# The sampling of the last five tiles: sums of weighted windows as matrix products with the identity, and another order of the last slots

## The chip, the cores and the metric

The kernel runs on one core of one Trainium2 chip, as a single launch. Its time is device microseconds (us), the median of three runs: 3848.34 us (3845.51 to 3851.66). The engines of the core that matter here are TensorE (PE in the profile, with its weight loads as PEld), VectorE (DVE), ScalarE (ACT), GpSimd (POOL) and SyncE (SP, which issues most of the DMAs). Each engine works through its own queue in order.

## The reference

The input is an image batch x of 4 x 64 x 64 pixels with 256 channels, in float32. Layer 0 is self-attention over the 4096 pixels of each image. Layer 1 is a block with deformable 3x3 sampling and an MLP:

```python
# layer 0
attention = softmax(q @ k.T);  x = gamma * (attention @ v) + x
# layer 1
h  = ln(x);  x_proj = h @ inproj_w + inproj_b
x1 = gelu(ln(depthwise3x3(h)))
offset, mask = x1 @ off_w + off_b, softmax(x1 @ mask_w + mask_b)   # per pixel: 16 groups, 9 points
val = bilinear samples of x_proj at (pixel + point + offset)
x = x + (sum over points of val * mask) @ outproj_w + outproj_b
x = x + gelu(ln(x) @ fc1_w + fc1_b) @ fc2_w + fc2_b
```

## The kernel before

A tile is 128 pixels (two image rows) with all 256 channels; there are 128 tiles. Attention works in 64 units of two tiles (b, u; UN = 64). The rest of layer 1 works in 65 pieces v = 0 to 64 (PN = 65): pieces 0 and 64 have one tile, all others two, so the last three pieces, 62, 63 and 64, have five tiles together.

The bilinear samples are not gathered one by one. As long as offsets stay within one pixel, each pixel's samples lie in a 5 x 5 window of x_proj. `plan` computes, for each pixel, window position and group, the weight `wn`. `sample` (line 1034) then computes, for each of a tile's five window rows r:

- `rows` (1039): SP loads the window row from DRAM, 128 pixels x 5 columns x 256 channels, unless an earlier tile loaded it; six such buffers exist;
- `times` (1042, product at 1047): DVE multiplies the window row by its weights, 128 x 1280 elements. Row 0 goes into a buffer with the tag "acc" (one of them), rows 1 to 4 into buffers with the tag "add" (two of them);
- `plus` (1054): DVE adds row r's product to row 0's, 128 x 1280 elements, four times a tile;
- `across` (1057): three DVE adds of 512, 256 and 256 elements per partition fold the five columns into `sp`, 128 x 256. At the end of a piece SP stores `sp` to `spd`.

`back` is the end of layer 1, in `finish` (line 1080): `turn` transposes `sp` on TensorE, `copy` (ACT), `project_out` (TensorE), `added` (DVE), `stats`, `shift`, `norm`, `turn2`, `scale`, then `hidden0` to `hidden7` (four matrix products each) with a `gelu` each on ACT, `narrowed0` and `narrowed1` (16 matrix products each, line 1141), and `end` (DVE, 1147), which also starts the store of the output. One more such round, `far` (1203), handles single points with large offsets, and `checks` tests whether a second pass is needed.

The order of the work is written out by hand. Slots are numbered; `WHEN` (324) gives each step a number within its slot, `LATE` (390) overrides it for the last slots (59 to 66), and `whole` (1326) sorts all steps by 60 x slot + number and emits them in this order. Each of TensorE, DVE, ACT and POOL then executes its instructions in exactly this order; SP's order is not fixed in this way. The numbers only set an order, they are not times. Piece v has its sampling and its back in slot v + 2, so pieces 62 to 64 belong to slots 64 to 66.

All results of TensorE that go through the PSUM tag "m" (transposes, products of `finish`, `plan` and `front`) share two buffers. Attention's scores use four PSUM buffers of their own, "e0" to "e3" (`e_tile`, 670), which are last used by the last attention unit.

Of the kernel before, what the change touches and what calls it, by code (L numbers as in the profile page):

```python
# [16 lines left out]
def tile_attention_dcnv3_block(  # L17
# [293 lines left out]
    def transposed(src, name, n=2, pool=None, tag="m"):  # L311

        pt = (pool or ps).tile([P, C // P, 256], F32, tag=tag, name=f"pt_{name}")
        for k in range(C // P):
            for i in range(n):
# [69 lines left out]
            "range": 12.0, "left": 12.1, "largest": 12.2,  # L385
# [6 lines left out]
            60: {"e2": 41.49, "w7": 44.5, "x2": 48.96, "w6": 49.61, "e3": 59.92, "w10": 62.77, "w4": 73.03,  # L392
                "x3": 83.29, "w11": 85.02, "w8": 89.86, "w12": 91.45, "w14": 94.26, "w13": 95.34,
                "w9": 113.4, "w15": 117.14},
            61: {"load": -3.2, "e0": 45.5, "x0": 51.27, "e1": 59.9, "x1": 71.66, "w0": 73.04, "w1": 76.59,
                "e2": 80.2, "w4": 82.06, "w3": 82.78, "x2": 83.76, "w10": 83.88, "w2": 86.39, "w7": 92.1,
                "w6": 100.44, "e3": 102.52, "w9": 103.15, "x3": 103.68, "w5": 104.24, "w12": 110.82,
                "w11": 114.27, "w14": 115.93, "w13": 116.02, "w8": 117.01, "w15": 117.71},
            62: {"load": 53.63, "e0": 66.06, "x0": 73.02, "e1": 78.84, "w0": 88.05, "w3": 100.69,
                "w2": 103.2, "x1": 106.97, "w5": 108.02, "w6": 113.39, "e2": 116.3, "w4": 117.55,  # L400
                "x2": 119.12, "w9": 122.0, "w1": 124.07, "e3": 124.61, "w10": 125.61, "w11": 131.23,
                "x3": 131.69, "w8": 135.71, "w13": 135.92, "w14": 137.46, "w12": 137.48, "w7": 138.87,
                "w15": 142.25},
            63: {"load": 45.22, "e0": 89.67, "x0": 91.49, "e1": 92.19, "w0": 98.07, "x1": 98.39, "w7": 99.54,
                "w1": 104.93, "e2": 104.94, "w3": 106.18, "w4": 108.57, "w2": 110.23, "x2": 111.63,
                "w9": 113.71, "e3": 117.35, "w11": 117.47, "x3": 117.74, "w12": 120.69, "w8": 121.81,
                "w13": 124.71, "w14": 130.05, "w5": 130.64, "w6": 131.24, "w10": 133.48, "w15": 135.85},
        },
        "sample": {
            60: {"rows14": 42.14, "rows13": 59.29, "across00": 61.86, "across01": 62.94, "across02": 65.9,  # L410
                "rows11": 71.88, "times11": 71.89, "rows10": 72.53, "times10": 72.54, "plus11": 73.67,
                "rows12": 73.82, "times12": 73.83, "times14": 79.95, "plus12": 81.1, "times13": 87.36,
                "plus13": 87.92, "plus14": 88.59, "across10": 90.04, "across11": 91.66, "across12": 96.83},
            61: {"rows04": -3.66, "rows03": 24.5, "rows14": 41.53, "rows00": 70.98, "times00": 70.99,
                "rows01": 71.16, "times01": 71.17, "rows02": 73.82, "times02": 73.83, "plus01": 79.14,
                "plus02": 80.53, "times03": 85.26, "times04": 85.98, "plus03": 86.15, "rows12": 91.45,
                "times12": 91.46, "plus04": 93.4, "across00": 99.51, "rows13": 100.36, "across01": 102.53,
                "across02": 108.03, "rows11": 112.36, "times11": 112.37, "rows10": 113.32, "times10": 113.33,
                "plus11": 114.34, "plus12": 118.64, "times13": 122.27, "times14": 123.0, "plus13": 126.65,
                "plus14": 129.62, "across10": 134.07, "across11": 141.77, "across12": 144.34},  # L420
            62: {"rows14": 72.21, "rows00": 117.68, "times00": 117.69, "rows03": 117.71, "rows01": 119.28,
                "times01": 119.29, "plus01": 121.78, "rows02": 124.59, "times02": 124.6, "rows04": 126.03,
                "plus02": 126.5, "times03": 126.6, "times04": 128.12, "plus03": 128.47, "plus04": 130.31,
                "rows11": 130.32, "times11": 130.33, "across00": 132.44, "across01": 135.0,
                "across02": 137.38, "rows10": 140.82, "times10": 140.83, "rows12": 141.57, "times12": 141.58,
                "plus11": 142.3, "times14": 145.21, "plus12": 150.77, "rows13": 152.98, "times13": 157.69,
                "plus13": 159.16, "plus14": 161.51, "across10": 165.15, "across11": 167.74,
                "across12": 169.62},
            63: {"rows13": 102.75, "rows04": 104.25, "rows00": 110.64, "times00": 110.65, "rows03": 112.68,
                "rows01": 114.51, "times01": 114.52, "rows02": 114.67, "times02": 114.68, "plus01": 115.3,  # L430
                "plus02": 119.19, "times03": 119.59, "times04": 121.51, "plus03": 121.85, "rows14": 125.54,
                "plus04": 128.4, "across00": 130.89, "rows12": 132.38, "across01": 132.39, "times12": 132.4,
                "rows11": 132.41, "times11": 132.42, "across02": 134.36, "rows10": 135.11, "times10": 135.12,
                "plus11": 137.85, "plus12": 145.42, "times13": 145.49, "times14": 146.33, "plus13": 149.57,
                "plus14": 150.93, "across10": 160.15, "across11": 162.44, "across12": 174.56},
            64: {"rows04": 62.71, "rows03": 94.46, "rows13": 135.97, "rows01": 136.98, "times01": 136.99,
                "rows00": 139.55, "times00": 139.56, "plus01": 142.22, "times03": 142.61, "rows02": 144.59,
                "times02": 144.6, "plus02": 145.58, "plus03": 151.96, "times04": 152.08, "rows11": 154.09,
                "times11": 154.1, "plus04": 154.11, "across00": 155.61, "rows12": 159.49, "times12": 159.5,
                "across01": 161.77, "across02": 171.41, "rows14": 175.68, "rows10": 177.57,  # L440
                "times10": 177.58, "plus11": 178.21, "times14": 179.49, "plus12": 179.56, "times13": 185.46,
                "plus13": 190.08, "plus14": 212.44, "across10": 220.75, "across11": 222.25,
                "across12": 230.44},
            65: {"rows14": 94.03, "rows03": 116.37, "rows04": 151.89, "rows00": 177.78, "times00": 177.79,
                "rows01": 179.39, "times01": 179.4, "plus01": 187.51, "rows02": 189.46, "times02": 189.47,
                "times03": 191.56, "plus02": 195.53, "plus03": 203.22, "times04": 205.67, "rows12": 213.72,
                "times12": 213.73, "plus04": 222.18, "across00": 222.92, "across01": 225.43, "rows13": 226.4,
                "across02": 230.02, "rows11": 231.43, "times11": 231.44, "rows10": 234.3, "times10": 234.31,
                "plus11": 236.93, "plus12": 241.12, "times13": 242.24, "times14": 247.32, "plus13": 248.9,
                "plus14": 251.64, "across10": 260.73, "across11": 267.14, "across12": 281.03},  # L450
            66: {"rows03": 182.99, "rows04": 183.57, "rows01": 292.3, "times01": 292.31, "rows00": 299.77,
                "times00": 299.78, "rows02": 302.28, "times02": 302.29, "plus01": 318.35, "plus02": 332.49,
                "times03": 351.38, "times04": 358.89, "plus03": 363.72, "plus04": 364.57, "across00": 372.87,
                "across01": 376.88, "across02": 380.09},
        },
        "plan": {
            60: {"tap3": 42.84, "tap4": 46.73, "tap5": 51.03, "tap6": 51.93, "tap7": 59.16, "tap8": 60.74,
                "turn": 60.98, "stats": 61.98, "shift": 66.63, "norm": 67.13, "turn2": 68.17, "gelu": 69.98,
                "heads0": 78.28, "bias0": 78.87, "heads1": 85.48, "bias1": 85.66, "hat0": 86.22,
                "hat2": 86.52, "mask_exp": 87.01, "hat1": 87.37, "sums": 88.24, "invert": 88.67,  # L460
                "nearer": 89.94, "weigh": 91.59, "near": 96.38, "carry": 96.51, "mask0": 97.55,
                "product0": 105.33, "y_copies0": 107.13, "mask1": 109.87, "y0": 114.77, "product1": 114.97,
                "y1": 120.64, "y_copies1": 123.19, "x_copies": 123.89, "x": 125.57, "count": 150.62,
                "bounds": 186.94},
# [569 lines left out]
    def sample(v, wns, sps):  # L1034
# [7 lines left out]
        def times(i, r):  # L1042
            if i == 0 and r == 0:
                sps[v] = p1.tile([P, 2, C], F32, tag="sp", name=f"sp_{n}")[:, :nt]
# [405 lines left out]
```

## Time and profile before

| | before |
|---|---|
| median of three runs | 3848.34 us |
| the profiled execution, its own time | 3846.97 us |
| its span in the trace | 3845.0 us |
| PE busy, instructions | 3770.7 us (98%), 20316 |
| DVE busy, instructions | 3421.7 us (89%), 6224 |
| ACT busy, instructions | 2201.8 us (57%), 4258 |
| L1047, products of `times` | 640 of 1485 ns |
| L1055, adds of `plus` | 512 of 1485 ns |

The span runs from the first to the last instruction of the profiled execution; its own time is 1.97 us longer. "Busy" is the time in which an engine has an instruction in it. Matrix products overlap in TensorE's pipeline, so their mean duration is longer than the distance from one to the next; where a product's price is wanted, it is read from the starts of a row of them.

### The profile page before, as it was taken

How to read it: one execution, taken by the hardware profiler on the slowest of the kernel's cores; microseconds unless marked ns; L12 is line 12 of the kernel's file. 1: busy time of each engine (PE TensorE's matmuls, PEld its weight loads, DVE VectorE, ACT ScalarE, POOL GpSimd, SP SyncE). 2: the span in 40 equal slices, each digit the busy share in tenths (PEclk: the TensorE clock that was granted, in tenths of full speed). 3: DMA queues.
4: the chain of work that ended last, by engine and by line, in shares of the span. 5: the costliest groups of instructions: out<-in, count | busy, mean ns of one | idle time of the engine just before them, and what ended most of it. 6: DMA issues, size and time to landing. Idle time of an engine off the chain costs nothing. (4 is left out here: it accounts for less than half of the span.)

```text
span 3845.0 us, 55916 instructions
## 1 busy us (share of the span) xinstructions
PE 3770.7 (98%) x20316; PEld 3117.3 (81%) x20316; DVE 3421.7 (89%) x6224; ACT 2201.8 (57%) x4258; POOL 317.6 (8%) x444
## 2 busy tenths in 40 slices
PE   8999999999999999999999999999999999999977
PEld 7788888888888888888888888888888888888755
DVE  2599899999999998998998998998999999999997
ACT  4556556556555565565565565565565566565533
POOL 1000000000000000000000000000000000000020
PEclk9999999999999999999999999999999999999979
DMA  5333333334343333333543333333343333332321
GB/s 150 91 104 89 94 101 90 96 94 137 99 110 95 97 91 94 100 94 88 150 111 91 106 91 91 104 89 95 106 123 102 95 87 92 87 94 75 99 79 51
DMA packets 231788, 378.01 MB, mean 98 GB/s; under 512 B 32880, under 2 KB 181936, under 8 KB 231504
## 3 DMA queue, kind: packets, MB, share of 16 engines
q1 hardware_dynamic: 221408, 367.46, 34.2%
q10 hardware_dynamic: 8512, 3.43, 0.4%
q8 instruction: 162, 2.65, 0.3%
q0 software_dynamic: 1584, 3.47, 0.3%
q14 instruction: 122, 1.00, 0.1%
HBM read 251.69 MB, written 122.56 MB: 97 GB/s over the span
## 5 line engine op out<-in xcount | busy, mean ns | idle before, releaser
L727 PE MATMUL acc<-V,ex 128*128 128x257 f32 x8192 | 1901.1, 382 | 1.6 <-ACT ex L715 1.5
L727 PEld LDWEIGHTS acc<-V,ex 128*128 128x128 f32 x8192 | 1532.1, 190 | 266.6 <-issue 65.5
L1047 DVE TENSOR_TENSOR pw<-win,wn 128x1280 f32<-128x1280 f32 x640 | 933.4, 1485 | 7.2 <-ACT wn L991 1.1
L1055 DVE TENSOR_TENSOR pw<-pw,pw 128x1280 f32<-128x1280 f32 x512 | 760.5, 1485 | 0.1
L715 ACT ACTIVATE ex<-e 128x512 f32<-128x512 f32 x1024 | 529.2, 602 | 65.3 <-PE e L702 60.7
L1124 PE MATMUL ph<-hT_b,f1w 128*128 128x256 f32 (+1 forms) x2080 | 498.8, 383 | 11.3 <-ACT gT L1132 7.5
L1141 PE MATMUL pmlp<-f2w,gT 128*128 128x256 f32 x2048 | 463.0, 379 | 0.3 <-DVE om L877 0.3
L1124 PEld LDWEIGHTS ph<-hT_b,f1w 128*128 128x128 f32 x2080 | 384.5, 191 | 91.2 <-issue 15.5
L831 DVE SCALAR_TENSOR_TENSOR cv<-hs,dw,cv 128x256 f32<-128x256 f32 (+1 forms) x1076 | 429.2, 466 | 7.9 <-ACT cv L827 1.3
L1141 PEld LDWEIGHTS pmlp<-f2w,gT 128*128 128x128 f32 x2048 | 384.1, 190 | 51.2 <-DVE om L877 0.8
L1132 ACT ACTIVATE gT<-ph,f1b 128x256 f32<-128x256 f32 (+1 forms) x520 | 236.9, 468 | 263.0 <-PE ph L1124 260.3
L288 ACT ACTIVATE xn_p<-pc,nm_p,rstd_p 128x256 f32<-128x256 f32 x128 | 65.5, 561 | 539.0 <-DVE nm_p L280 539.0
L702 PE MATMUL e<-qs,kT 32*128 32x256 f32 x4096 | 297.1, 401 | 0.7 <-ACT ex L715 0.7
L702 PEld LDWEIGHTS e<-qs,kT 32*128 32x128 f32 x4096 | 187.1, 184 | 72.7 <-issue 63.3
L715 ACT ACT_TABLE_LOAD x185 | 237.4, 1283 | 3.1
L274 POOL TENSOR_SCALAR rstd_p<-mv_p 128x2 f32<-128x2 f32 (+1 forms) x65 | 76.2, 1173 | 1700.4 <-DVE mv_p L272 1665.4
L868 PE MATMUL po<-om_w,ge 128*128 128x432 f32 x512 | 197.6, 528 | 0.7 <-ACT ge L861 0.7
L957 DVE TENSOR_TENSOR pr<-hat 128x1296 f32<-128x1296 f32 x128 | 192.7, 1506 | 0.7 <-DVE nm_b L280 0.5
L1132 ACT ACT_TABLE_LOAD x124 | 159.1, 1283 | 6.4 <-PE ph L1124 4.2
L861 ACT ACTIVATE ge<-pt_p,bd,gd 128x256 f32<-128x256 f32 (+1 forms) x130 | 66.0, 559 | 157.8 <-PE pt_p L316 157.8
L877 DVE TENSOR_TENSOR om<-po,om_b 128x432 f32<-128x432 f32 x128 | 77.3, 605 | 87.9 <-PE po L868 87.9
L868 PEld LDWEIGHTS po<-om_w,ge 128*128 128x128 f32 x512 | 97.7, 191 | 70.9 <-issue 64.0
(215 smaller groups left out, 3823.6 us busy)
## 6 DMA issues: line engine op xcount, KB each, us to landing
win<-xp SPq DMA_DIRECT2D x536, 320.0 KB, 4.1
omd<-om SPq DMA_DIRECT2D x63, 432.0 KB, 2.5
xs<-in_x_dram SPq DMA_DIRECT2D x64, 256.0 KB, 5.4
x<-in_x_dram SPq DMA_DIRECT2D x64, 256.0 KB, 2.7
x1d<-x SPq DMA_DIRECT2D x64, 256.0 KB, 3.2
xp<-xq SPq DMA_DIRECT2D x128, 128.0 KB, 2.4
x1b<-x1d SPq DMA_DIRECT2D x63, 256.0 KB, 2.8
spd<-sp SPq DMA_DIRECT2D x63, 256.0 KB, 2.1
```

The source lines that it names most:

```text
L702: nc.tensor.matmul(es[r][:, jj, :], lhsT=self.kT[2 * g + jj][rows4(r), :], rhs=self.qs[rows4(r), :], start=True, stop=not self.general,)
L715: nc.scalar.activation(ex, self.es[r], AF.Exp)
L727: nc.tensor.matmul(self.acc[i], lhsT=ex[:, jj, i * P : (i + 1) * P], rhs=V[t // 2][:, t % 2, :], start=(g == 0 and r == 0 and jj == 0), st ...
L831: nc.vector.scalar_tensor_tensor(dst, src, dw[:, k, j : j + 1], dst, ALU.mult, ALU.add)
L868: nc.tensor.matmul(st["po", i], lhsT=st["ge"][:, k, i * P : (i + 1) * P], rhs=om_w[:, k, :], start=(k == 0), stop=(k == 1),)
L877: nc.vector.tensor_add(st["om"][:, i, :], st["po", i], om_b)
L957: nc.vector.tensor_mul(pr.rearrange("p a b c d g -> p a b (c d g)"), hat[:, :, i, 1, :].unsqueeze(1).to_broadcast([P, 3, 3, S]), hat[:, :, ...
L1047: nc.vector.tensor_mul(st[r].rearrange("p d (g c) -> p (d g) c", c=GC), src.rearrange("p d (g c) -> p (d g) c", c=GC), wns[v][:, i, r] .re ...
L1055: nc.vector.tensor_add(st[0], st[0], st[r])
L1124: nc.tensor.matmul(ph[:, :m], lhsT=f1w[:, k, c * P : (c + 1) * P], rhs=st["hT"][:, k, :m], start=(k == 0), stop=(k == 1),)
L1132: nc.scalar.activation(st["gT"][:, c, :m], st["ph", c][:, :m], AF.Gelu, bias=f1b[:, c : c + 1])
L1141: nc.tensor.matmul(po, lhsT=st["gT"][:, c, i * P : (i + 1) * P], rhs=f2w[:, c, :], start=(c == 0), stop=(c == NH - 1),)
```

## The change

For pieces 62, 63 and 64 (`v >= UN - 2`), the sums over the window are made in another way. Of the five products of a tile, rows 1 and 2 are added on DVE in place (`pair`, j = 1), and so are rows 3 and 4 (`pair`, j = 3). The three row buffers that are left (1, 0 and 3), each of five columns, are added by TensorE: `sum_up` multiplies each column by the identity and accumulates all 15 products in one PSUM tile, which uses one of attention's score buffers. ACT copies the result to `sp` (`summed`). `plus` and `across` are not called for these pieces. Their steps have a stage of their own, "summing". In `times`, `sp` is now allocated at the first call for a piece, whichever row that is.

```diff
         def times(i, r):
-            if i == 0 and r == 0:
+            if v not in sps:
                 sps[v] = p1.tile([P, 2, C], F32, tag="sp", name=f"sp_{n}")[:, :nt]
...
+        def pair(j):
+            nc.vector.tensor_add(st[j], st[j], st[j + 1])
+
+        def sum_up(i, j):
+            if j == 1:
+                st["sum", i] = ps_e.tile([P, 2, C], F32, tag=f"e{2 * (v % 2) + i}", name=f"sum_{n}_{i}")[:, 0, :]
+            for d in range(WIN):
+                nc.tensor.matmul(
+                    st["sum", i], lhsT=ident, rhs=st[j][:, d, :],
+                    start=(j == 1 and d == 0), stop=(j == 3 and d == WIN - 1),
+                )
+
+        def summed(i):
+            nc.scalar.copy(sps[v][:, i, :], st["sum", i])
+            if i == nt - 1:
+                nc.sync.dma_start(spt_[:, g0 : g0 + nt], sps[v])
+
         d = {}
+        if v >= UN - 2:
+            for i in range(nt):
+                for r in range(WIN):
+                    d[f"rows{i}{r}"] = lambda i=i, r=r: rows(i, r)
+                    d[f"times{i}{r}"] = lambda i=i, r=r: times(i, r)
+                for j in (1, 3):
+                    d[f"pair{i}{j}"] = lambda j=j: pair(j)
+                for j in (1, 0, 3):
+                    d[f"sum{i}{j}"] = lambda i=i, j=j: sum_up(i, j)
+                d[f"summed{i}"] = lambda i=i: summed(i)
+            return d
...
-            put(v + 2, "sample", sample(v, wns, sps))
+            put(v + 2, "sample" if v < UN - 2 else "summing", sample(v, wns, sps))
```

The second part replaces nearly the whole of `LATE`: every stage of slots 59 to 66 gets new numbers, so the order of all steps in the last slots changes, attention's included. As an example, here are the numbers of piece 63's sampling (slot 65) and of the checks:

```diff
-            65: {"rows14": 94.03, "rows03": 116.37, "rows04": 151.89, "rows00": 177.78, "times00": 177.79,
-                "rows01": 179.39, "times01": 179.4, "plus01": 187.51, "rows02": 189.46, "times02": 189.47,
...
+            65: {"rows04": 101.89, "rows03": 178.02, "rows13": 232.6, "rows02": 250.39, "times02": 250.4,
+                "rows01": 254.69, "times01": 254.7, "pair01": 261.82, "rows14": 262.32, "rows00": 267.01,
+                "times00": 267.02, "times03": 267.13, "sum01": 267.42, "times04": 270.89, "sum00": 283.46,
+                "pair03": 287.04, "rows11": 288.53, "times11": 288.54, "sum03": 294.71, "rows12": 320.51,
+                "times12": 320.52, "pair11": 346.58, "sum11": 348.47, "rows10": 353.1, "times10": 353.11,
+                "times14": 354.54, "sum10": 357.52, "times13": 357.91, "pair13": 358.79, "summed0": 364.31,
+                "sum13": 364.33, "summed1": 367.57},
...
-            66: {"range": 395.84, "left": 485.76, "largest": 510.45},
+            66: {"range": 530.02, "left": 563.34, "largest": 1080.93},
```

Sorted, the new order of TensorE from piece 63's last sum to the end is: the sum; `turn` of far and of 63; `project_out` of far and of 63; `narrowed0` and `narrowed1` of 62; `turn2`, eight `hidden`, `narrowed0` and `narrowed1` of 63; `turn2` of far; the first sum of the last tile; two `hidden` of far; the second sum; two `hidden` of far; the third sum; one `hidden` of far; `turn` of 64; one `hidden` of far; `project_out` of 64; two `hidden`, then `narrowed0` of far; `turn2`, eight `hidden` and `narrowed0` of 64; `largest` of the checks. Before, `largest` (two small products) stood between `turn2` and the first `hidden` of 64.

## The prediction

> **What bounds the kernel now.** I read the page first (PE 98% busy, DVE 89%), then the busy time by stretches, cut where the work changes: the last attention product ends at 3668.1 us, the last sum of the last tile's sampling at 3815.5.
>
> ```profile
> core 0: us, PE busy (x) PEld busy (x) DVE busy (x) ACT busy (x) POOL busy (x), PEclk, DMA share, GB/s
> 3500.00:3600.00 100.00, 100.00 (x550) 82.47 (x552) 94.50 (x175) 51.27 (x103) 10.81 (x12) 1.00 0.31 84
> 3600.00:3668.10 68.10, 65.61 (x345) 52.29 (x337) 66.59 (x114) 39.38 (x69) 6.47 (x7) 1.00 0.32 86
> 3668.10:3815.50 147.40, 105.24 (x420) 79.58 (x419) 140.67 (x288) 54.93 (x121) 24.21 (x26) 0.84 0.27 77
> 3815.50:3845.00 29.50, 18.89 (x96) 14.71 (x94) 5.79 (x24) 9.89 (x24) 1.89 (x3) 0.84 0.06 19
> ```
>
> While attention runs, PE is full. In the third stretch, where all five changed tiles are sampled, DVE is idle for only 6.7 us of 147.4, PE for 42.2, at a mean clock of 0.84. In the last stretch PE leads again. So DVE time taken out of the third stretch is worth its full length, as long as PE keeps up there.
>
> **What goes from DVE.** The timeline of DVE shows start, duration and line; the price of an instruction is the distance to the next start.
>
> ```profile
> 3787.19 0.69 DVE L1060 TENSOR_TENSOR pw<-pw 128x512 f32<-128x512 f32 x1
> 3787.79 0.60 DVE L949 TENSOR_TENSOR hat<-hat,mk 128x432 f32<-128x432 f32 x1
> 3788.31 0.42 DVE L1062 TENSOR_TENSOR pw<-pw 128x256 f32<-128x256 f32 x1
> 3788.64 0.69 DVE L1113 TENSOR_TENSOR x1b<-x1b,f2b 128x512 f32<-128x512 f32 x1
> 3789.24 0.42 DVE L1064 TENSOR_TENSOR sp<-pw 128x256 f32<-128x256 f32 x1
> 3789.58 1.51 DVE L957 TENSOR_TENSOR pr<-hat 128x1296 f32<-128x1296 f32 x1
> ...
> 3804.54 1.49 DVE L1055 TENSOR_TENSOR pw<-pw,pw 128x1280 f32<-128x1280 f32 x1
> 3805.94 0.19 DVE L932 TENSOR_TENSOR least<-least,ms 128x32 f32<-128x32 f32 x1
> ```
>
> The `across` adds cost 0.60 + 0.33 + 0.34 = 1.27 us a tile, one `plus` 1.40. A tile has five products before and after; four `plus` and three `across` become two `pair` of the same size as `plus`. Saved: 2 x 1.40 + 1.27 = 4.07 us a tile, 20.4 us for five.
>
> **What comes to PE.** Fifteen products a tile, 75 in all, 128x256 in float32, the form of L1141 and L1099. Timeline of PE, with the idle time before a row in brackets:
>
> ```profile
> 3687.89 3.78 PE L1099 MATMUL pout<-ow,sT 128*128 128x256 f32 x8
> ...
> 3776.39 5.45 PE L1124 MATMUL ph<-hT_b,f1w 128*128 128x256 f32 x24 [1.85 <-ACT gT L1132]
> 3781.68 7.07 PE L1141 MATMUL pmlp<-f2w,gT 128*128 128x256 f32 x32
> 3788.59 0.27 PE L316 MATMUL pt_s<-ident,sp 128*128 128x128 f32 x1
> ```
>
> Thirty-two products from 3781.68 to 3788.59 are 0.216 us each, so five columns cost 1.08 us and all 75 cost 16.2. But the eight at 3687.89, which start 1.6 us after an idle time of 6.3 us (DVE's sum was late), take until 3691.47, 0.447 each. [...] I take 0.216 for the sums after the fourth gap below and count one half-rate period after each gap of 4 us or more.
>
> Does it fit? In the third stretch PE's products at 0.216 (and in proportion to their columns) come to about 86 us; the other 19 of the 105 busy are low clock. With the 16.2, and with `narrowed` steps that the new order sorts ahead of the last sum, PE has about 104 to 108 us of work up to that sum, and DVE 140.7 - 20.4 = 120.3. PE is slack on average, not everywhere.
>
> **The walk through the new order.** I sorted the steps and added the prices above on both engines.
>
> - Up to the end of attention both orders hold nearly the same: 168.9 us of PE steps against 170.9 from the same start. Worth up to 2 us, counted as 0, because DVE, which is 98% busy from 3600 on, decides what follows.
> - From 3668 to piece 63's last sum DVE leads. Between the same point of piece 61's sampling (done at 3668.5) and piece 63's last `pair`, DVE has 101 us of work; with 2 us of idle time that `pair` ends at 3771. On the way PE has waits of about 5 us (for the last attention tile's norm), 4 us (for 63's taps) and 4 us (for 64's norm). The half clock after the first two costs PE's slack alone. After the third, about 3748, it would push on DVE.
> - From 3772 PE leads. Its queue from there to the end, from the rows: turns and projections 3.3, two `narrowed` 6.9, turn 0.4, eight `hidden` 7.2, two `narrowed` 6.9, turn 0.2, three sums 3.2, far's `hidden` 4.6, turn and projection 1.1, far's `narrowed` 3.5, turn 0.2, `hidden` 4.7, `narrowed` 3.7: 46 us. DVE, with some 27 us of work up to the last tile's `pair`, must wait in between: its `end` of 63 stands ahead of the last `times`, and 63's `narrowed` isn't done before 3797.
>
> The last rows of the chain of waits (start, length) give the prices of that tail:
>
> ```profile
> 3798.71 7.20 PE ph L1124 x32
> ...
> 3821.60 5.42 PE pmlp_f L1141 x16
> ...
> 3832.84 3.69 PE pmlp L1141 x16
> ```
>
> PE's small waits after 3797 sum to 3.4 us before (for ACT copies, norms, gelu tables); I keep 3.4. So PE ends at 3772 + 46 + 3.4 = 3821.4, against 3836.5: **15.1 us earlier**. What follows it (0.4 us `end`, the store, about 8 us to the end of the span) stays.
>
> **Edits with a small price.** (1) ACT gets five copies of 128x256; the row of the same form (L1093) has 0.37 us, 1.9 in all. ACT is 37% busy there; only the last one is on the path, but three `across` (1.27) leave it, so copy plus last five products (1.08 + 0.37) is about even. (2) Waits added on DVE: "add" has two buffers; after each `pair` the second next product needs the buffer that the `sum` still reads, nine times in all; the single "acc" buffer likewise waits for the middle sum. Behind the waiting product stand all of DVE's taps, norms and `end`s. The new order leaves 1.7 us (63's row 2, second tile) to several us between `pair` and that product, against 1.08 for the sum: from 0 to 9 x 1 us; I take 1, as most have 3 us. (3) PSUM: the sums use attention's score buffers, free by then; nothing. (4) `largest` moves from ahead of the last eight `hidden` to the end: 0.6 us leave the path (inside the 15.1), and its answer comes some 1.5 us after the last `end`, beside the output's store, which takes 3.0 us to land: nothing; 1 us if that cover is gone. (5) Loads of windows: every new one is requested before or as soon as one of six buffers is read out, on SP, which has 4.3 us median to landing; 62's row 4 is the tightest: its buffer comes free with row 1's product, some 9 us of DVE work ahead of its use. Cost 0 to 3 us (SP may stand at another wait), taken as 0. (6) `spd` is stored after ACT's copy; nobody reads these tiles from DRAM.
>
> **Sum.** 20.4 saved on DVE, of which the PE tail gives about 5 back: 15 us with (2) inside the rounding. The profiled execution goes from 3847.0 to 3832; the median shown lies 1.4 us above it, so the forecast is **3833**.
>
> **Rivals.**
> - *DVE all the way* (0.24): PE keeps warm and its tail fits; 20.4 minus about 1: 3829. For it: PE has 42 us idle. Against: `end` of 63 ahead of the last products.
> - *The clock takes a part* (0.18): PE falls to half rate after several gaps (before, it lost 19 us that way, hidden by DVE's lead) and pushes DVE back by 6 to 8 us: 3840. For it: waits of 4 to 5 us remain. Against: more PE work fills them.
> - *The order brings more* (0.10): the 13.7 us in which DVE is not busy from 3500 to 3815 and the table loads in the tail (2.8 us on the chain about 3817) shrink too: 3824.
> - *The hand-over decides* (0.07): PE works in order, so a sum can stand behind a `hidden` that waits for ACT. Nine times DVE needs the "add" buffer that a sum reads; above 20.4 / 9 = 2.3 us a time the saving is gone. At 3.5 us it is 31.5 - 20.4: 11 us slower, 3859. Before, sums waited 6.3 us in one such place; against it, the order puts two or three DVE steps between.
> - *Hardly anything arrives* (0.06): the same wait at about 2 us: 3846.
>
> **How the numbers follow.** The forecast has 0.35. A measurement of this kernel can tell about 0.2%, 7.7 us. Faster by more: forecast, DVE all the way, the order, and three quarters of the clock's case: 0.82. Within: the rest of that and the small remainder, 0.11. Slower: 0.07. The range 3823 to 3843 leaves out the hand-over and part of the last rival.
>
> **What would show it.** DVE: 25 instructions and about 20 us fewer. PE: 75 more, and in the last 170 us less idle time than 42 us. If the walk is right, DVE waits for PE at the `end` of 63 for several us, and PE's last 46 us run almost without a gap. A low PE clock late (after 3748) speaks for the clock; DVE waits at L1047 on PE of over 2 us speak for the hand-over. I am wrong if DVE remains busy to the last `pair`, or if attention ends more than 4 us earlier or later than 3668.

## The result and the profile after

| | before | after |
|---|---|---|
| median of 13 runs each | 3848.70 us (3845.51 to 3852.93) | 3837.92 us (3836.23 to 3843.61) |
| ratio after to before, 95% interval | | 0.9973 [0.9966, 0.998] |
| profiled execution, own time | 3846.97 us | 3837.92 us |
| its span | 3845.0 us | 3835.8 us |

The change saves about 10 us. The forecast was 3833 us with a range of 3823 to 3843: the direction and the range hold, the gain is 10 to 11 us where 15 were expected. First the page of the kernel after, its busy times and two of its groups (busy time and mean ns of one, then the idle time before them):

```profile
PE 3789.8 (99%) x20466; PEld 3139.2 (82%) x20466; DVE 3401.7 (89%) x6199; ACT 2199.0 (57%) x4261; POOL 312.9 (8%) x444
...
L1064 DVE TENSOR_TENSOR pw<-win,wn 128x1280 f32<-128x1280 f32 x640 | 933.8, 1486 | 9.5 <-ACT wn L1008 1.9
L1072 DVE TENSOR_TENSOR pw<-pw,pw 128x1280 f32<-128x1280 f32 x492 | 731.9, 1488 | 0.1
```

DVE has 25 instructions and 20.0 us less, as forecast; L1072 (`plus`) has lost its 20. But PE has 150 rows more, not 75. Now the kernel after by stretches, cut as the prediction cut the kernel before: at the end of the last attention product, now 3663.2, and at the end of the last tile's last sum, now 3807.3:

```profile
core 0: us, PE busy (x) PEld busy (x) DVE busy (x) ACT busy (x) POOL busy (x), PEclk, DMA share, GB/s
...
3600.00:3663.20 63.20, 63.08 (x335) 51.34 (x334) 62.22 (x118) 30.59 (x60) 8.41 (x11) 1.00 0.31 82
3663.20:3807.30 144.10, 128.13 (x580) 103.55 (x580) 126.83 (x279) 63.55 (x135) 23.63 (x26) 0.98 0.29 81
3807.30:3835.80 28.50, 16.72 (x93) 13.25 (x91) 3.31 (x11) 7.07 (x20) 1.88 (x3) 0.88 0.05 17
```

In the middle stretch DVE is idle for 17.3 us where it was idle for 6.7, and PE for 16.0 where it was idle for 42.2; the mean PE clock is 0.98 instead of 0.84. Neither engine has much room left. The clock record of the trace says the same in another way: between the end of attention and the last `narrowed` product PE ran at half clock for 51.2 us before (in four pieces of 10.2, 23.9, 13.7 and 3.4), and for 6.8 us after.

The timeline of PE after gives the price of the sums (start, duration, line, shape, number of rows):

```profile
3682.70 1.40 PE L316 MATMUL pt_f<-ident,xn_f 128*128 128x128 f32 x4 [3.02 <-ACT xn_f L288]
...
3767.85 2.32 PE L1093 MATMUL sum<-pw,ident 128*128 128x256 f32 x10
3770.01 1.03 PE L1170 MATMUL ph<-hT_b,f1w 128*128 128x256 f32 x4
3770.87 2.32 PE L1093 MATMUL sum<-pw,ident 128*128 128x256 f32 x10
```

One `sum_up` has five calls of the product and ten rows in the trace; from 3767.85 to 3770.01 it takes 2.16 us, so 0.216 us a row and 0.43 us a call. The 75 calls cost 32.4 us at full clock, not 16.2. The first row shows the longest wait of PE in the whole of the changed part, 3.02 us for the last attention tile's norm; the 6.8 us of half clock begin in its last third of a microsecond.

The timeline of DVE after, from piece 63's last `pair` on:

```profile
3768.59 1.49 DVE L1087 TENSOR_TENSOR pw<-pw,pw 128x1280 f32<-128x1280 f32 x1
...
3799.01 0.69 DVE L1193 TENSOR_TENSOR x1b<-x1b,pmlp 128x512 f32<-128x512 f32 x1 [2.00 <-PE pmlp L1187]
3799.62 1.49 DVE L1064 TENSOR_TENSOR pw<-win,wn 128x1280 f32<-128x1280 f32 x1
3801.39 1.49 DVE L1064 TENSOR_TENSOR pw<-win,wn 128x1280 f32<-128x1280 f32 x1 [0.29 <-PE sum L1093]
3802.92 1.49 DVE L1087 TENSOR_TENSOR pw<-pw,pw 128x1280 f32<-128x1280 f32 x1
...
3824.51 0.42 DVE L1193 TENSOR_TENSOR x1b<-x1b,pmlp 128x256 f32<-128x256 f32 x1 [8.54 <-PE pmlp L1187]
```

The last `pair` of 63 ends at 3770.1 (3771 was forecast). DVE then waits for PE at the `end` of 63, and the last tile's last `pair` ends at 3804.4, only 0.7 us before PE takes up the sum that reads it (3805.13). PE leads here, but DVE is close behind.

The chain of waits after shows the tail (start, length, engine, line, rows):

```profile
3771.03 2.17 PE sum L1093 x10
...
3776.87 6.91 PE pmlp L1187 x32
...
3799.19 2.16 PE sum L1093 x10
3801.35 0.89 PE ph_f L1170 x8
3802.24 2.16 PE sum L1093 x10
3804.41 0.89 PE ph_f L1170 x8
3805.30 2.16 PE sum L1093 x10
...
3820.75 3.72 PE pmlp L1187 x16
3824.47 0.54 PE pt_any L1441 x4
```

From 3771 to 3824 the chain is PE's own queue with ACT and DVE in small steps between. The three sums of the last tile take 6.5 us of it, and `largest` now stands at its end.

**Where the 10 us are.** Single executions differ by some us, and that shift arises in the first 250 us of the span. So profiles are compared here from a common point late in the run, the start of attention's unit 59, the first that the new numbers touch (row 7553 of 8192 of L727 or L744, near 3420 us in all of them). The 3168.4 us ahead of it, from row 513 on, are the same to 0.1 us in every profile (row 513 starts at 251.5 us before and at 252.1 after). From the common point to the end of the span it takes 425.1 us before and 415.4 after, 9.8 less before rounding:

| from the common point | before | after | difference |
|---|---|---|---|
| to piece 63's sampling done (last `across`; after: last sum's copy) | 369.8 | 353.1 | -16.7 |
| from there to the end of the last `narrowed` product | 46.9 | 50.9 | +4.0 |
| from there to the end of the span | 8.5 | 11.4 | +2.9 |

The first line has the size of the saving on DVE of the four tiles of pieces 62 and 63 (4 x 4.07 = 16.3): in this stretch DVE is busy for 353.3 us before and 338.3 after, while its idle time hardly changes (16.5 and 14.9). The other two lines give part of it back. The experiments ask which terms these are, and whether DVE or PE now sets the end.

### The profile page after: what moved, and what is told of

The parts are those of the page before. It is cut to its first block, busy times and chain, and to the rows that moved or that the text cites. A ratio compares the mean times of both kernels' runs of the same rounds, so it can differ in the third digit from the quotient of the medians.

```text
span 3835.8 us, 56185 instructions
## 1 busy us (share of the span) xinstructions
PE 3789.8 (99%) x20466; PEld 3139.2 (82%) x20466; DVE 3401.7 (89%) x6199; ACT 2199.0 (57%) x4261; POOL 312.9 (8%) x444
## 4 chain that ended last, share of the span: by engine, by line
PE 96%; DVE 3%; DMA 1%; ACT 0%; issue 0%; SPq 0%; ACTq 0%; DVEq 0%
PE acc L744 46%; PE ph L1170 11%; PE pmlp L1187 11%; PE e L719 7%; PE po L885 5%; PE pout L1145 3%; PE pp L801 3%; PE pv L651 3%; PE pkq L630 1%; DVE pw L1064 1%; PE pt_p L316 1%; PE pc L861 1%; PE pt_f L316 1%; PE pt_s L316 1%; PE pt_b L316 1%; PE pt_x L316 1%
## 5 line engine op out<-in xcount | busy, mean ns | idle before, releaser
L744 PE MATMUL acc<-V,ex 128*128 128x257 f32 x8192 | 1900.9, 382 | 0.2
L744 PEld LDWEIGHTS acc<-V,ex 128*128 128x128 f32 x8192 | 1532.0, 190 | 264.5 <-issue 64.8
L1072 DVE TENSOR_TENSOR pw<-pw,pw 128x1280 f32<-128x1280 f32 x492 | 731.9, 1488 | 0.1
```

Of the source, the lines that this page charges most:

```text
L744: nc.tensor.matmul(self.acc[i], lhsT=ex[:, jj, i * P : (i + 1) * P], rhs=V[t // 2][:, t % 2, :], start=(g == 0 and r == 0 and jj == 0), st ...
L1072: nc.vector.tensor_add(st[0], st[0], st[r])
```

## The experiments

Ratios are against the kernel before, run beside each kernel on the same chip. Between two experiments a difference of 1 to 2 us is smaller than these intervals, so those are read from the common point, in one profile each.

### `largest` ahead of the last eight `hidden` again

```diff
-            66: {"range": 530.02, "left": 563.34, "largest": 1080.93},
+            66: {"range": 530.02, "left": 563.34, "largest": 700.0},
```

> The changed kernel with one number altered: the checks' last step (two small products, a reduction, the answer that all engines read) stands ahead of the last eight hidden steps again, as before the change, instead of behind the last narrowed. In the changed kernel 11.3 us pass from the last narrowed product to the end of the span, in the kernel before 8.5. Theory A (the answer is the last thing that all engines wait for): the stretch behind the last narrowed shrinks to about 8.5 us and 0.5 us of products come ahead of it, so the kernel is about 2.3 us faster than the changed one (about 3835.5, ratio to the kernel before near 0.9967). Theory B, that of the prediction (the answer lies beside the output's store): no difference beyond 0.5 us, about 3838.

Measured: 3835.95 us (3834.41 to 3837.61), ratio 0.9968 [0.9956, 0.998]. From the common point 413.2 us, 2.2 less than after. The timeline of PE of this kernel:

```profile
3814.42 0.60 PE L1441 MATMUL pt_any<-ident,tot 128*1 128x128 f32 x4 [0.30 <-DVE f_x_f L1193]
3815.02 4.73 PE L1170 MATMUL ph<-hT_b,f1w 128*128 128x128 f32 x32
3819.76 3.72 PE L1187 MATMUL pmlp<-f2w,gT 128*128 128x256 f32 x16
```

The products of `largest` cost 0.6 us in the queue here. But from the end of the last `narrowed` (3823.48) to the end of the span (3832.4) it takes 8.9 us instead of 11.4. The rows of the line that reads the answer tell why (PEldq and DVEq are the instruction queues of TensorE and VectorE; shortest, median and longest in ns, then the first and last start in us). First the kernel after:

```profile
L1454 PEldq TENSOR_LOAD <-res_any x1: 533/533/533, 3825.7 to 3825.7; - x1
```

Then this kernel:

```profile
L1454 PEldq TENSOR_LOAD <-res_any x1: 482/482/482, 3820.2 to 3820.2; - x1
L1454 DVEq TENSOR_LOAD <-res_any x1: 547/547/547, 3823.5 to 3823.5; - x1
```

After the change all five engines read it into a register at 3825.7 us, behind the last `end`; here SyncE and GpSimd read it at 3815.7, ScalarE at 3819.8 and TensorE at 3820.2, beside running work. Only VectorE reads it at the very end (3823.5). So the move of `largest` costs 2 us, and most of the +2.9 in the table is this.

### One column of five in every sum

```diff
-            for d in range(WIN):
+            cols = 1
+            for d in range(cols):
...
-                    start=(j == 1 and d == 0), stop=(j == 3 and d == WIN - 1),
+                    start=(j == 1 and d == 0), stop=(j == 3 and d == cols - 1),
```

> The changed kernel, but TensorE adds only the first of the five columns of each of a tile's three buffers: 3 products instead of 15, the other twelve sums are left out, so the output is not the reference's. DVE's work and all orders stay. A column takes two rows of TensorE in the trace (0.43 us), so TensorE has 26 us less in the five tiles, 5.2 of them in the last tile. Theory A (the sums cost twice the 16.2 us of the prediction and TensorE leads from piece 63's sampling to the end): faster than the changed kernel by 5.2 us for the last tile and by some more for piece 63, 7 to 10 us in all, about 3829. Theory B (DVE leads throughout, and TensorE's share of the sums hides): 0 to 2 us.

Measured: 3836.18 us (3835.23 to 3840.45), ratio 0.9969 [0.9957, 0.9981]; from the common point 414.3, only 1.1 less than after, though 26 us of products are gone from PE. Timeline of PE:

```profile
3773.10 0.70 PE L1094 MATMUL sum<-pw,ident 128*128 128x256 f32 x2 [1.07 <-DVE pw L1087]
...
3807.55 0.70 PE L1094 MATMUL sum<-pw,ident 128*128 128x256 f32 x2 [1.73 <-DVE pw L1087]
```

Now PE waits for DVE's `pair` at both sums that matter, the last of 63 and the last of 64. PE's half clock grew from 6.8 to 23.9 us. So the products after the change lie almost wholly in PE time that would otherwise be idle or at half clock. Taken alone this says that DVE leads.

### One `pair` left out in pieces 62 and 63

```diff
-            nc.vector.tensor_add(st[j], st[j], st[j + 1])
+            if j == 1 or v == UN:
+                nc.vector.tensor_add(st[j], st[j], st[j + 1])
```

> The changed kernel, but in pieces 62 and 63 the second pair (row 4 added to row 3) is left out, so row 4 is missing from these four tiles' sums; TensorE's work and all orders are unchanged. DVE has 4 x 1.40 = 5.6 us less ahead of piece 63's last sum and the same work behind it. Theory A (DVE leads up to piece 63's last sum): nearly all of it arrives, 4 to 5.6 us faster than the changed kernel, 3832 to 3834. Theory B (TensorE, whose sums take twice what the prediction gave them, leads from about 3745 on): under 2 us, 3836 to 3838.

Measured: 3837.52 us (3834.72 to 3839.2), ratio 0.9972 [0.996, 0.9983]; from the common point 414.8, 0.6 less than after, though 5.6 us are gone from DVE. First a row of DVE's timeline, then two of PE's:

```profile
3758.16 1.49 DVE L1064 TENSOR_TENSOR pw<-win,wn 128x1280 f32<-128x1280 f32 x1 [1.97 <-PE sum L1094]
```

```profile
3764.69 2.32 PE L1094 MATMUL sum<-pw,ident 128*128 128x256 f32 x10
...
3767.71 2.32 PE L1094 MATMUL sum<-pw,ident 128*128 128x256 f32 x10
```

DVE now waits 1.97 us where a product needs the buffer that a sum still reads, and PE takes its sums without a wait for DVE: from 3744 to 3771 it has no gap. The last sum of 63 starts 349.6 us after the common point, against 350.4. Taken alone this says that PE leads.

### Both cuts together

The edits are those of the last two experiments in one kernel.

> Both cuts in one kernel: TensorE adds one column of five in all five tiles (26 us less), and in pieces 62 and 63 the second pair is left out (DVE 5.6 us less); the output lacks what is left out. Each cut alone moved piece 63's last sum by only 1.6 and 0.9 us (counted from the same attention product near 3475 us), and the time by 1 to 2 us. Theory A (DVE and TensorE arrive at piece 63's last sum together, so neither cut alone can help): together they move that sum by 4 us or more and the kernel is 3 to 6 us faster than the changed one, 3832 to 3835. Theory B (something else leads there, ACT's gelus or the window loads): again under 2 us, 3836 to 3838.

Measured: 3830.9 us (3828.79 to 3834.37), ratio 0.9954 [0.9941, 0.9968]; from the common point 407.4, which is 7.9 less than after. The sum of the two single effects is 1.7. The last sum of 63 starts 345.9 us after the common point, 4.5 earlier than after. Its row in the timeline of PE, below the longest of PE's waits close ahead of it:

```profile
3767.09 1.13 PE L1172 MATMUL ph<-hT_b,f1w 128*128 128x256 f32 x4 [1.71 <-ACT gT L1180]
...
3769.35 0.59 PE L1095 MATMUL sum<-pw,ident 128*128 128x256 f32 x2
```

So up to 63's last sum DVE and PE arrive together: neither alone is the bound, and work taken from one alone moves that sum by 0.8 us (DVE) or 1.6 us (PE, 348.8 in its profile), since the other stops it. With both cut PE takes this sum without a wait for DVE, and its longest wait close ahead is 1.71 us for one of ACT's `gelu` steps: a third chain begins to show. A comparison that cuts only one of two such engines shows next to no effect for each of them (here 0.6 and 1.1 us).

### One column of five in the last tile alone

```diff
+            cols = 1 if v == UN else WIN
+            for d in range(cols):
```

> The changed kernel, but only in the very last tile (piece 64) TensorE adds one column of five and leaves the other four out; the first four changed tiles are summed in full, so TensorE's clock can't drop ahead of the tail as it did when all five tiles were cut. TensorE has 5.2 us less behind piece 63's last narrowed. Theory A (from piece 63's last sum on TensorE leads, so each of its products there counts): 3 to 5 us faster than the changed kernel, 3833 to 3835. Theory B (the last tile's chain of products, pair, copy and projection leads, and TensorE's sums lie beside it): 0 to 1.5 us, 3836.5 to 3838.

Measured: 3836.77 us (3835.0 to 3841.01), ratio 0.9972 [0.9961, 0.9983]; from the common point 413.8, 1.6 less than after, where 5.2 us left PE's queue (3 x (2.16 - 0.43)). Timeline of PE:

```profile
3803.01 0.70 PE L1094 MATMUL sum<-pw,ident 128*128 128x256 f32 x2 [1.73 <-DVE pw L1087]
...
3805.79 2.06 PE L1146 MATMUL pout<-ow,sT 128*128 128x256 f32 x4
```

1.73 us of the 5.2 turn into a wait for DVE's last `pair`, and the projection behind it runs at half clock (3804.4 to 3807.8 in the clock record): 2.06 us against 1.13 after. DVE's chain from the `end` of 63 over two products to that `pair` is the next bound, 0.7 us behind PE, as its timeline after showed.

### The new order with the old sums

```diff
+    LATE["sample"].update({
...
+        65: {'times00': 250.4, 'times01': 254.7, 'plus01': 261.82, 'times02': 267.02,
...
+    })
...
-        if v >= UN - 2:
+        if v > UN:
...
-            put(v + 2, "sample" if v < UN - 2 else "summing", sample(v, wns, sps))
+            put(v + 2, "sample", sample(v, wns, sps))
```

The steps of the old sampling stand, in their own order, at the places that the new steps had.

> The changed kernel's new order of the last slots, but the last five tiles are summed as before, by four plus and three across on DVE; these take the places in the order at which the new steps stood. DVE has 20 us more than in the changed kernel, TensorE 32 us less. Theory A (the gain is that of the moved sums): DVE leads again and the time is near that of the kernel before, 3845 to 3855. Theory B (the renewed order itself brings the gain): 3838 to 3842.

Measured: 3862.7 us (3861.23 to 3866.03), ratio 1.0039 [1.0025, 1.0052]: slower than before. The busy time of this kernel by stretches, with the columns as above:

```profile
3700.00:3740.00 40.00, 23.06 (x72) 15.72 (x72) 37.23 (x85) 12.70 (x23) 5.65 (x7) 0.78 0.28 67
3740.00:3780.00 40.00, 28.15 (x104) 20.50 (x104) 39.09 (x68) 18.04 (x38) 5.06 (x6) 0.80 0.41 110
3780.00:3820.00 40.00, 29.00 (x122) 23.52 (x120) 29.08 (x60) 9.35 (x24) 2.81 (x5) 0.83 0.08 28
```

DVE is full to 3780, PE is idle and at a low clock beside it, and then, from 3780 to 3820, PE falls behind on the rest with 11 us idle. With this placement the order alone brings nothing. It also answers a smaller question: here attention's last product ends as early as after the change (242.9 us behind the common point in both, 248.4 before), so that early end is no gain by itself.

### The old order with the new sums

```diff
+    LATE["summing"] = {
...
+        65: {'times01': 177.79, 'times02': 179.4, 'pair01': 187.51, 'times00': 189.47,
+            'times03': 191.56, 'times04': 195.53, 'pair03': 203.22, 'sum01': 187.513,
+            'sum00': 189.473, 'sum03': 203.223, 'summed0': 203.224,
...
+    }
```

All other numbers are those of the kernel before. DVE's seven steps of a tile stand at the first seven of the twelve places that it had, each sum right behind the step that it needs.

> The sums on TensorE with the order of the kernel before: each tile's five products and two pair steps take the first seven of the twelve places that the old steps had, each sum follows its pair or product at once, and the copy follows the last sum. Theory A (the moved sums need an order made for them, since TensorE works its queue in order and meets sums whose products are late): a smaller gain than the changed kernel's 10.4, 3840 to 3848. Theory B (the order matters little): 3836 to 3840. If TensorE waits for DVE at the sums in many places, it can be slower than the kernel before.

Measured: 3885.1 us (3885.1 to 3885.31), ratio 1.0095 [1.008, 1.0111]. The waits of PE, then of DVE, in this kernel from 3600 us on (us in total, times, longest):

```profile
PE sum L1091 <- DVE pw L1085: 25.8, 6, 11.9
```

```profile
DVE x1b L1191 <- PE pmlp L1185: 25.1, 3, 9.6
DVE x1b L1150 <- PE pout L1143: 18.1, 2, 12.2
```

PE works in order. It stands at sums whose `pair` is late, for 25.8 us, and behind them stand the products that DVE's `end` and `added` need; so DVE stands in turn. This is what the prediction's hand-over rival described (PE behind late sums, to the point of being slower than before), and it is what the new order avoids. For comparison, DVE's waits in the kernel after, from 3400 us on:

```profile
DVE x1b L1193 <- PE pmlp L1187: 14.0, 5, 8.5
...
DVE pw L1064 <- PE sum L1093: 1.5, 2, 1.2
```

So sums and order are worth something only together. Both of these experiments use a placement of mine; that no other old-order placement could gain isn't shown.

### Three attempts at a better tail

All three keep `largest` ahead, as in the first experiment. The first also takes the last attention tile's `shift` ahead of the `end` that stood before it, for PE's 3.02 us wait, and leaves out the early loading of ACT's exp table in the last slots:

```diff
-            64: {"inverse": 124.15, "residual": 131.68, "stats": 136.56, "shift": 150.51, "norm": 152.62,
+            64: {"inverse": 124.15, "residual": 131.68, "stats": 136.56, "shift": 149.63, "norm": 152.62,
...
-                put(s, "tables", {k: lambda f=f: ready(f) for k, f in TABLES.items()})
+                put(s, "tables", {k: lambda f=f: ready(f) for k, f in TABLES.items() if k != "exp" or s < UN - 2})
```

> The changed kernel with the checks' last step ahead (as in e1), the shift of the last attention tile's norm ahead of piece 59's end step on DVE instead of behind it and a plus, and without the two last warm-ups of the exp table, after which no exp comes. In the changed kernel TensorE waits 3.0 us for that norm near 3680 us and then runs 6.8 us at half clock. Theory A (TensorE and DVE both gain there: TensorE's wait and the low clock, DVE's 2 us wait for the products behind them): 1.5 to 4 us faster than e1, 3832 to 3834.5. Theory B (the gain is lost again at the next wait, for piece 63's taps): no difference to e1 beyond 1 us.

The second samples the last tile on DVE as before the change, with the `end` of 63 between its steps and the last tile's turn and projection behind far's `hidden`:

```diff
-                "raised": 496.31, "gelu3": 503.87, "narrowed0": 508.49, "narrowed1": 513.64, "end": 541.07},
+                "raised": 496.31, "gelu3": 503.87, "narrowed0": 508.49, "narrowed1": 513.64, "end": 514.2},
...
+    LATE["back"][66].update({"turn": 620.0, "copy": 621.0, "project_out": 622.0, "added": 623.0, "stats": 624.0})
...
-        if v >= UN - 2:
+        if UN - 2 <= v < UN:
```

> The changed kernel with three edits of the tail: the last tile (piece 64) is summed on DVE as before the change, since DVE waits for TensorE there anyway; piece 63's end step stands in the middle of that tile's products; the turn and projection of 64 stand behind far's hidden steps; and the checks' last step stands ahead of the last eight hidden steps. Against the changed kernel TensorE has 6.5 us less in the tail and DVE 4.1 us more. Theory A (TensorE leads in the tail, and the checks' answer costs 2 us at the end): about 2 us for the checks and 3 to 5 for the tail, 3831 to 3833, below both kernels. Theory B (the last tile's chain leads): the tail gains nothing or loses up to 3 us, 3835 to 3839.

The third has the edits of both.

> The edits of e7 (last tile's sums on DVE, checks ahead) and of e11 (early shift, no late exp warm-ups) together. In e7 TensorE waits 2.5 us in far's hidden steps for two table loads on ACT that the warm-up causes. Theory A (TensorE leads in the tail): 2 to 5 us faster than e7, 3830 to 3833, the fastest of all. Theory B (the last tile's chain leads): within 1 us of e7.

| | median (range), us | ratio to before | from the common point |
|---|---|---|---|
| `largest` ahead alone | 3835.95 (3834.41 to 3837.61) | 0.9968 [0.9956, 0.998] | 413.2 |
| `largest` ahead, early `shift`, no exp load | 3834.26 (3832.84 to 3835.3) | 0.9963 [0.9949, 0.9976] | 412.4 |
| `largest` ahead, last tile on DVE | 3835.24 (3833.86 to 3835.75) | 0.9964 [0.9951, 0.9978] | 412.0 |
| all of these | 3835.54 (3833.83 to 3837.71) | 0.9967 [0.9955, 0.9979] | 412.9 |

In the timeline of PE with the early `shift`:

```profile
3680.80 0.63 PE L316 MATMUL pt_f<-ident,xn_f 128*128 128x128 f32 x4 [0.87 <-ACT xn_f L288]
...
3687.67 0.90 PE L316 MATMUL pt_s<-ident,sp 128*128 128x128 f32 x3 [3.38 <-DVE sp L1081]
```

The wait of 3.02 us went down to 0.87, and the next one, for DVE's `sp`, up from 0.91 to 3.38: DVE's own work sets the time there. And in the timeline of PE with all edits:

```profile
3808.88 0.66 PE L316 MATMUL pt_s<-ident,sp 128*128 128x128 f32 x2 [2.26 <-DVE safe L1429]
...
3811.87 5.24 PE L1192 MATMUL pmlp_f<-f2w,gT_f 128*128 128x256 f32 x16
```

There the last tile's sum on DVE is late by 2.26 us, and far's `narrowed` behind it takes 5.24 us where the second attempt has 3.62, with the clock at half for 6.8 us in this profile's record. All four versions lie below the kernel after by medians, by 2 to 4 us; which of them is best, these intervals can't tell. The last tile on DVE and all edits together miss the gain that their theories A gave them (3831 to 3833 and 3830 to 3833).

## Why the prediction was right, step by step

- **DVE's saving.** 25 instructions and 20.4 us were forecast, 25 and 20.0 measured. Right; piece 63's last `pair` ended 1.5 us ahead of its forecast, counted from the common point.
- **PE's price: the term that was mis-sized.** "Thirty-two products from 3781.68 to 3788.59 are 0.216 us each, so five columns cost 1.08 us and all 75 cost 16.2." The thirty-two were rows of the trace, and one call of these float32 products makes two rows (75 calls of sums, 150 rows more): the two `narrowed` there are 16 calls. (The description of the kernel counts rows too where it gives a `hidden` four products and a `narrowed` 16; the code makes two and eight calls.) Five columns cost 2.16 us and all 75 cost 32.4.
- **PE's end.** Counted from the common point it was forecast at 401.5 us and came at 404.0, 2.5 later. The end of 63's last sum is 0.4 of this: the `pair` came 1.5 earlier, PE took the sum up 0.8 later, and the sum took 1.1 more. From there the three sums of the tail took 6.5 us instead of 3.2; PE's small waits were 1.5 us (0.66, 0.30, 0.55), not 3.4; the other steps took 0.7 more.
- **What the right price would have changed.** The forecast would have been near 3837 instead of 3833, and so next to the 3838 measured, but partly by luck: the waits and `largest` were off in opposite directions, by 1.9 and 2.9 us. And sums at the forecast's own price would not have gained the 3.3 us either: the last tile's much cheaper sums of the fifth experiment gain only 1.6, since DVE's last `pair` is then late. "DVE, with some 27 us of work up to the last tile's `pair`, must wait" held with 0.7 us to spare: the slack of the engine that waits should have been worked out as well.
- **"PE is slack on average."** With the doubled price it is not: 104 to 108 us of PE work from the end of attention to the last tile's last sum were forecast, and PE was busy for 128.1. Its idle time in the sampling stretch fell from 42.2 to 16.0 us, and DVE and PE reach 63's last sum together (the two single cuts and the double one). That DVE sets the pace up to there was half of it. That DVE's pace was kept all the same, with 16 us more of sums than forecast, was luck as far as the forecast goes: PE lost far less time at half clock than it had counted with (next point).
- **The clock.** Three gaps of 5, 4 and 4 us with a half-clock period each were forecast, their harm doubtful. One gap of 3.02 us and one period of 6.8 us were measured. PE's idle time in the middle stretch fell from 42.2 to 16.0 us, and PE spent 44 us less at half clock (51.2 - 6.8), worth up to half of that in PE work by an estimate from the rows (0.447 us each behind the gap of 6.28 us before, 0.216 at full clock), against the 16 us that the sums cost more than forecast. No run holds the clock fixed, so this account is read from the records and not shown by itself. Counting one half-rate period after each gap of 4 us or more was the author's estimate for this order, not a measured limit. The profiles show this: before, half clock began inside PE's gaps of 6.28, 11.98 and 4.53 us (at 3682.1, 3702.6 and 3743.5), the 24 products behind a gap of 1.85 us took 0.22 us each, and a fourth period began at 3822.0, where the longest gap close ahead was 0.84; after, one began inside the gap of 3.02. The price of 0.216 us a row held for the sums: all 15 lie between 3702.2 and 3807.5, behind the period at half clock, which ended at 3689.2. That more work on PE could mean less half clock the prediction says only in a clause of a rival ("more PE work fills them").
- **Edit (4), `largest` at the end.** "Nothing; 1 us if that cover is gone" was wrong: 2.2 us. It weighed the answer against the store's landing, and left out that all five engines read that answer, after the change at 3825.7 us behind the last `end`.
- **Edits (1), (2), (3), (5), (6).** Hand-over of the buffers 1.5 us at `times` (1 forecast); no wait of DVE for a window's load; nothing seen at the others.
- **The sum.** -15.1 us forecast, -9.8 measured from the common point: 2.5 from PE's later end and 2.9 behind it make up the difference, to 0.1 us.
- **What I called a sign of being wrong.** Attention ended 4.9 us earlier (3663.2), more than the 4 us allowed. (From the common point it is 5.5: 2.4 are idle time of PE that is gone, and 1.7 are eight rows of `hidden` that now stand behind attention's last product.) The new order with the old sums has the same early end and is 15 us slower than before; the sign was badly chosen. The other two signs came: DVE waits at the `end` of 63, though for 2.0 us and not for several, and PE's last stretch runs almost without a gap.
- **The rivals.** DVE all the way fell with PE's price; the clock took less than before, not more (6.8 us at half clock, 51.2 before); the order alone brought nothing in the one placement tried; the hand-over is real, and appears when the sums stand in the old order.

Still open: how much the early end of attention contributes, which wasn't isolated; and whether sums in a form other than float32 would cost less, which wasn't tried.

## What to carry to other kernels

Price an instruction by what one call leaves in the trace, counting calls in the code against rows in the same stretch, before the price is carried to a new place. Where two engines take turns, cut the work of each alone and of both: two small effects and a large one together (here 0.6 and 1.1 us, then 7.9) mean a balance, and it takes both to move the end, as it did here. Products put where TensorE was idle can be nearly free (26 us of them cost 1.1 here), but each needs a place in the order at which its input is ready: in the old order TensorE stood at the sums for 25.8 us, with the products behind them.

## What the hardware showed that was not expected

- Work taken from TensorE hardly shortened the run: without 26 us of products its time at half clock rose from 6.8 to 23.9 us, and the run was 1.1 us shorter, counted from the common point. How much of the rest is the clock and how much DVE's pace isn't separated. In the clock records the periods at half clock from 3550 us to the last product were 10.2, 23.9, 13.7 and 3.4 us long before the change and 6.8 us after it; the 6.8 began inside a gap of 3.02 us.
- The length of one gap doesn't sort these periods; the busy time of PE over 3.41 us, the shortest of them, does it better. The profiles before and after, cut into steps of that length in phase with the clock's changes, from 3550 us to the last product, have 147 full-clock steps. The four in which PE was busy for 1.36 us or less were followed by half clock. Of the next three, that of 1.86 us was and those of 1.57 and 1.83 us were not, and none of the 140 with 1.87 us or more was. Half clock ended behind five steps, with 2.95 to 3.41 us of work, and went on behind twelve, with up to 2.97. These are counts from two profiles; no run varies the busy time by itself. Timeline of PE before the change, where the 3.4 us at half clock begin at 3822.0 and PE was busy for 1.86 us of the step ahead:

```profile
3818.88 0.71 PE L1124 MATMUL ph_f<-hT_bf,f1w 128*128 128x128 f32 x4 [0.51 <-DVE x1b L1106]
3820.43 0.71 PE L1124 MATMUL ph_f<-hT_bf,f1w 128*128 128x128 f32 x4 [0.84 <-ACT gT_f L1132]
3821.60 5.41 PE L1141 MATMUL pmlp_f<-f2w,gT_f 128*128 128x256 f32 x16 [0.46 <-ACT gT_f L1132]
```

- The answer of a check, read by all five engines at the end of the program, cost 2.2 us here when it came after the last step (415.4 us from the common point, 413.2 with it ahead), while the products that make it take 0.6 us.
